# A four-layer graph network on one core: layer 0's table moved to the front of the prologue, edges loaded with groups on partitions

## The chip, the core and the metric

The kernel runs on one core of a Trainium2 chip. A core has five engines that run side by side, each with its own queue of instructions that it works off strictly in order: PE (TensorE, matrix products and transposes), DVE (VectorE), ACT (ScalarE), POOL (GpSimd) and SP (SyncE, which here issues nearly all DMAs). They wait for each other and for DMAs by semaphores. The metric is the device time of one execution in microseconds (us). The profile is one execution taken by the hardware profiler; its span runs from the first to the last instruction.

## The reference

A graph of N = 12,500 nodes and E = 212,500 directed edges, sorted by destination, goes through four layers. Each layer computes `h = relu(layernorm(x))` and adds a message-passing term to `x`:

```
x = x + L0(h, edge_attr_16)   # 4-head attention: softmax over a node's incoming edges
x = x + L1(h, edge_weight1)   # weighted sum over incoming edges, gelu, linear, gelu
x = x + L2(h, edge_attr_9)    # tensor product of rows with edge features, sum
x = x + L3(h)                 # mean over incoming edges, two linears, batch norm
```

Layer 0 is the one that the change is about:

```
Wh = (h @ W.T).reshape(N, 4, 32)
attn = (concat([Wh[src], Wh[dst]], -1) * a).sum(-1)        # per edge and head
attn = leaky_relu(attn, 0.2) + edge_feat @ W_e.T
alpha = segment_softmax(attn, dst)
out = layer_norm(gelu(segment_sum(alpha * Wh[src], dst)))
```

The score splits into a part of the source row and a part of the destination row, so that one table row per node holds what a source gives: 128 numbers of `Wh` and 4 of its part of the score.

## The kernel before

The edges are cut into 208 groups of 1,024 (`GE`; 128 partitions times `T` = 8 slots; the last group is partly filled). Because edges are sorted, the destinations of a group lie in a window of 128 nodes from a first node `base` on.

Before layer 0 there is a prologue (lines 198 to 955), which has no order written out by hand: a scheduler orders each engine's instructions there, and pools of memory decide what may overlap. It has these parts, in this order in the text:

1. Edges (lines 217 to 333). `di` (destinations) and `si` (sources) are loaded as tiles of 128 partitions x 208 groups x 8 slots by `load_edges`, whose pieces are 8 numbers, 32 bytes, each. `ext` takes the largest and smallest destination of each group on each partition, POOL's `partition_all_reduce` makes the maximum over partitions (`red`), `base` comes from it, and `rel` is destination minus `base`. A padded copy of `dst` is made in DRAM (`dpad`), and three shifted copies `seq` of it are read back, from which `bad`, `below` and `units` are made: tests of whether the graph fits the fast path, and where each window of edges begins. `least` and `end` are limits per group, filled by some 60 small memsets. Last, `rel` is transposed in 13 pieces and stored as `rel16` in DRAM.
2. Weights and constants (lines 338 to 423): W0 and the attention vectors become `WE` (128 x 136), the other weights are transposed, `TP` and `mixer` are filled.
3. Layer 0's table (lines 918 to 954): in 25 batches of 4 blocks of 128 nodes, with pools two deep, rows of x are loaded (`xt`), normalised (`norm`, DVE with one square root on ACT), put through relu on ACT, transposed on PE (`pt`), copied by ACT (`hT`), multiplied by `WE` on PE (`pw`), copied out by ACT (`tt`) and DVE (`sd`), and stored by SP as `tab0` (132 numbers a row) and `sdt` (the destination parts, split in three bf16 numbers).

Then layer 0's loop (lines 956 to 1137) runs over the groups in an order written out by hand. For a group g, `load(g)` has SP load edge features, `rel16` rows (`rb`) and a window of `sdt` (`sdw`); `logits(g)` has POOL issue eight indirect DMAs (`gather`, line 661) that fetch 1,024 rows of `tab0` into a row buffer `X`, makes a one-hot matrix `ST` from `rb` (line 1004, DVE), multiplies it by `sdw` on PE, and sums the scores `at` (lines 1010 to 1013, DVE), which SP stores to `lgt` (line 1015). `weights` computes the softmax for four groups at a time. Seven groups later (`LAG`) `spread_out` multiplies the rows by the weights (`msg`, line 1078, DVE) and PE sums them per node (`pag`). A row buffer is free again after that; there are 15 (`LAG + 8`). They lie in the loop's own pool `e0`, whose memory was the prologue's before. In between, the loop makes steps of `Slots` (tables for layers 1 and 3) and of `node0` (the end of layer 0 for a batch of nodes, stored as `xtab` and `htab`).

Layer 1 starts with a load of all edge weights `eww` (lines 1221 to 1230, again by 32-byte pieces), a memset of `tabS` and gathers of `htab`. Its pools take over the memory of layer 0's loop. Layers 2 and 3 follow in the same way.

Of the kernel before, what the change touches and what calls it, by code (L numbers as in the profile page):

```python
# [26 lines left out]
P = 128  # L27
# [66 lines left out]
def gnn_kernel(ctx: ExitStack, tc, x, src, dst, ef16, ef9, ew, W0, We0, a0, lns, lnb, W1, b1,  # L94
# [102 lines left out]

    si = cst.tile([P, NG, T], I, name="si")
    rel = cst.tile([P, NG, T], F, name="rel")
# [5 lines left out]
    early = ExitStack()  # L205
    tmp = early.enter_context(tc.tile_pool(name="acp", bufs=1))
# [6 lines left out]
    TOT = PADF + NG * GE + P  # L213
    NSG = NG // SG
    NK = -(-NB // NBK)
# [5 lines left out]
    with tc.tile_pool(name="ed", bufs=1) as ep:  # L221
        di = ep.tile([P, NG, T], I, name="di")
        load_edges(di, dst, 0, NG, N, 1)
        load_edges(si, src, 0, NG, 0, 1)
        df = ep.tile([P, NG, T], F, name="df")
        vec.tensor_copy(df, di)

        ends = ep.tile([1, max(PADF, TOT - PADF - E)], I, name="ends")
        vec.memset(ends, -1)
        nc.sync.dma_start(dpad[None, :PADF], ends[:, :PADF])  # L230
        ends2 = ep.tile([1, TOT - PADF - E], I, name="ends2")
        vec.memset(ends2, N)
        nc.sync.dma_start(dpad[None, PADF + E :], ends2)
        cut = max(k for k in range(1, P + 1) if E % k == 0)
        nc.sync.dma_start(dpad[PADF : PADF + E].rearrange("(a b) -> a b", a=cut), dst.rearrange("(a b) -> a b", a=cut))
        ext = ep.tile([P, 2, NG + 1], F, name="ext")
        vec.memset(ext[:, :, NG:], 0.0)
        vec.tensor_reduce(ext[:, 0, :NG], df, AX.X, ALU.max)
        vec.tensor_reduce(ext[:, 1, :NG], df, AX.X, ALU.min)
        vec.tensor_scalar_mul(ext[:, 1, :NG], ext[:, 1, :NG], -1.0)  # L240

        seq = [ep.tile([P, NG * T], I, name=f"seq{k}") for k in (0, 1, 2)]
        for t, k in zip(seq, (0, 1, HALO)):
            nc.sync.dma_start(t, windows(dpad, PADF + k, P, NG * T, NG * T))
        bad = [ep.tile([P, NG * T], F, name=f"bad{k}") for k in (0, 1)]
        vec.tensor_tensor(bad[0], seq[2], seq[0], ALU.is_le)
        vec.tensor_scalar(bad[1], seq[0], float(N), None, op0=ALU.is_lt)
        vec.tensor_tensor(bad[0], bad[0], bad[1], ALU.mult)
        vec.tensor_tensor(bad[1], seq[1], seq[0], ALU.is_lt)
        vec.tensor_tensor(bad[0], bad[0], bad[1], ALU.max)  # L250
        vec.tensor_reduce(ext[:, 0, NG:], bad[0], AX.X, ALU.max)
        red = ep.tile([P, 2, NG + 1], F, name="red")
        pool.partition_all_reduce(red, ext, P, bass_isa.ReduceOp.max)
        base = ep.tile([P, NG], F, name="base")
        vec.tensor_scalar_mul(base, red[:, 1, :NG], -1.0)
        vec.tensor_copy(bi, base)
        vec.tensor_tensor(rel, df, base[:, :, None].to_broadcast([P, NG, T]), ALU.subtract)
        vec.tensor_scalar(widx, base, pcol, None, op0=ALU.add)
        span = ep.tile([P, NG], F, name="span")
        vec.tensor_tensor(span, red[:, 0, :NG], base, ALU.subtract)  # L260
        vec.tensor_copy(xall, span)
        vec.tensor_scalar(xall, xall, 7, None, op0=ALU.logical_shift_right)
        vec.tensor_scalar(xall, xall, 1.0, None, op0=ALU.add)
        vec.tensor_scalar(bi3, base, float(BM), None, op0=ALU.min)
        vec.tensor_scalar(bir, bi, RW - 1, None, op0=ALU.bitwise_and)

        last = base[:, G0 - GM : G0, None].to_broadcast([P, GM, T])
        vec.tensor_tensor(relx, rel[:, G0 - GM : G0, :], last, ALU.add)
        vec.tensor_scalar(relx, relx, W0_ * P - 0.5, 4.0 * P, op0=ALU.is_gt, op1=ALU.mult)
        vec.tensor_tensor(relx, relx, rel[:, G0 - GM : G0, :], ALU.add)  # L270
        most = ep.tile([P, 1], F, name="most")
        vec.tensor_reduce(most, span, AX.X, ALU.max)
        worst = ep.tile([P, 1], F, name="worst")
        vec.scalar_tensor_tensor(worst, red[:, 0, NG:], float(W), most, op0=ALU.mult, op1=ALU.max)

        least = ep.tile([P, NG], F, name="least")
        vec.memset(least, 0.0)
        for k, g in enumerate(done):
            if g + 1 < NG:
                vec.memset(least[:, g + 1 :], float(min(NBK * P * (k + 1), N)))  # L280
        vec.memset(least[:, G0:], float(W0_ * P))
        for k, g in enumerate(done):
            if g + 1 >= G0 and g + 1 < NG:
                vec.memset(least[:, g + 1 :], float(min(NBK * P * (k + 1), N)))
        vec.tensor_tensor(least, base, least, ALU.is_lt)

        end = ep.tile([P, NG], F, name="end")
        vec.memset(end, float(RW - W))
        for k, g in enumerate(done):
            if g + 6 < NG:  # L290
                vec.memset(end[:, g + 6 :], float(NBK * P * (k + 1) + RW - W))
        vec.tensor_tensor(end, base, end, ALU.is_gt)
        vec.tensor_tensor(least, least, end, ALU.max)

        UP = NG * T // P
        edge = ep.tile([P, 2, NW], F, name="edge")
        vec.tensor_copy(edge[:, 0, :], wnode)
        vec.tensor_scalar(edge[:, 1, :], wnode, float(P), float(N), op0=ALU.add, op1=ALU.min)
        below = ep.tile([P, 2, NW, UP], F, name="below")
        for k, at in enumerate((P - 1, 0)):  # L300
            unit = seq[0].rearrange("p (u e) -> p u e", e=P)[:, :, at]
            vec.tensor_tensor(below[:, k], unit[:, None, :].to_broadcast([P, NW, UP]),
                              edge[:, k, :, None].to_broadcast([P, NW, UP]), ALU.is_lt)
        units = ep.tile([P, 2, NW], F, name="units")
        vec.tensor_reduce(units, below, AX.X, ALU.add)
        with tc.tile_pool(name="bgp", bufs=1, space=PSUM) as pp:
            pun = pp.tile([P, 2, NW], F, name="pun")
            pe.matmul(pun.rearrange("p k w -> p (k w)"), ones, units.rearrange("p k w -> p (k w)"),
                      start=True, stop=True)
            vec.tensor_scalar(begin, pun[:, 0, :], float(P), float(E - UN * P), op0=ALU.mult, op1=ALU.min)  # L310
            vec.tensor_copy(units[:, 1, :], pun[:, 1, :])
            vec.tensor_tensor(units[:, 0, :], units[:, 1, :], pun[:, 0, :], ALU.subtract)
        vec.tensor_scalar(units[:, 0, :], units[:, 0, :], UN + 0.5, None, op0=ALU.is_gt)
        many = ep.tile([P, 1], F, name="many")
        vec.tensor_reduce(many, units[:, 0, :], AX.X, ALU.max)
        vec.scalar_tensor_tensor(worst, many, float(W), worst, op0=ALU.mult, op1=ALU.max)
        vec.tensor_scalar(many, base[:, G0 - 1 : G0], BM + 0.5, None, op0=ALU.is_gt)
        vec.scalar_tensor_tensor(worst, many, float(W), worst, op0=ALU.mult, op1=ALU.max)
        vec.tensor_scalar(many, red[:, 0, G0 - GM - 1 : G0 - GM], W0_ * P - 0.5, None, op0=ALU.is_gt)
        vec.scalar_tensor_tensor(worst, many, float(W), worst, op0=ALU.mult, op1=ALU.max)  # L320
        late = ep.tile([P, 1], F, name="late")
        vec.tensor_reduce(late, least, AX.X, ALU.max)
        vec.scalar_tensor_tensor(worst, late, float(W), worst, op0=ALU.mult, op1=ALU.max)
        vec.tensor_copy(rough, worst)
        relf = rel.rearrange("p g t -> p (g t)")
        with tc.tile_pool(name="edp", bufs=2, space=PSUM) as pp:
            for c in range(0, NG * T, P):
                n = min(P, NG * T - c)
                prl = pp.tile([P, P], F, name="prl")
                pe.transpose(prl[:n, :], relf[:, c : c + n], ident)  # L330
                rl = ep.tile([P, P], B16, name="rl", bufs=2)
                vec.tensor_copy(rl[:n, :], prl[:n, :])
                nc.sync.dma_start(rel16[c : c + n, :], rl[:n, :])
    ef16f = ef16.rearrange("e f -> (e f)")
    ef9f = ef9.rearrange("e f -> (e f)")


    WE = cst.tile([P, P + 2 * H], F, name="WE")
    W1T = cst.tile([P, P], F, name="W1T")
    WlT = cst.tile([P, P], F, name="WlT")  # L340
    WrT = cst.tile([P, P], F, name="WrT")
# [578 lines left out]
    with tc.tile_pool(name="p0", bufs=2) as sp, tc.tile_pool(name="p0p", bufs=2, space=PSUM) as pp:  # L920
# [5 lines left out]
        for b0, nb in batches(4):  # L926
# [3 lines left out]
            for _ in norm(sp, xt, nb, h):  # L930
                pass
# [833 lines left out]
```

## Time and profile before

| what | us |
|---|---|
| median of 3 runs (7439.46 to 7453.02) | 7448.18 |
| profiled execution | 7429.66 |
| its span | 7427.8 |
| prologue: start to the first gather of layer 0 | 0 to 231.9 |
| of it the table of layer 0 (first load of x to first gather) | 99.9 to 231.9 |
| layer 0's loop: first gather to last sum of messages | 231.9 to 2495 |
| layer 1's first gather | 2524.9 |

All times inside the profiled execution are counted from the start of its span. A row of a timeline gives the start and the duration of an instruction, its engine, its line and operation, and in brackets how long the engine had been idle and what ended that. "SPq" is the time in which SP issues a DMA, not the time of the transfer. A row of a table of windows gives the stretch, its length, the busy time of PE, of PE's weight loads, of DVE, ACT and POOL with the instructions in brackets, then the clock that was granted to PE (1.00 is full speed), the mean busy share of the DMA engines and the GB/s that they moved. Some records of matrix products and of other instructions are missing, so counts are taken from DMA issues.

### The profile page before, as it was taken

Reading aid. Unit: us, or ns where it says so; the run is one execution under the profiler, and the core shown is the slowest. Engines: PE = TensorE matmul, PEld = TensorE weight load, DVE = VectorE, ACT = ScalarE, POOL = GpSimd, SP = SyncE. Lnnn points to the kernel's source line nnn. Section 1 sums busy time; section 2 is a strip of 40 time slices with the busy share of each in tenths; the row PEclk is TensorE's granted clock in tenths of the full one; section 3 lists DMA queues with packets and bytes.
Section 4 is the critical chain, followed back from the end, with each engine's and each line's share of the span. In section 5 each row is a group of like instructions: output and inputs, shape, how many; then the busy total and the mean of one; then the engine's idle time right before and its main releaser. Section 6 shows DMA issues by size and latency. Waiting matters only on the chain.

```text
span 7427.8 us, 119421 instructions
## 1 busy us (share of the span) xinstructions
PE 5056.1 (68%) x39957; PEld 3687.5 (50%) x39958; DVE 5283.1 (71%) x10506; ACT 2841.6 (38%) x7693; POOL 5145.2 (69%) x5372
## 2 busy tenths in 40 slices
PE   3344445444444499888987787778787758788787
PEld 2344444344444366555656777777777732222222
DVE  5678888888888445544448999999999944545454
ACT  1244444444444234434443333333333314444443
POOL 0577777777775377777737777777777767777772
PEclk8566666666666699999987888888888868888887
DMA  5444444444443433333322222222222244344333
GB/s 84 96 105 103 104 106 105 107 106 103 105 105 94 84 88 96 95 90 94 93 72 57 67 71 66 68 69 67 70 69 66 69 126 105 105 106 105 102 103 108
DMA packets 741279, 674.54 MB, mean 91 GB/s; under 512 B 341283, under 2 KB 629398, under 8 KB 740631
## 3 DMA queue, kind: packets, MB, share of 16 engines
q0 software_dynamic: 186624, 382.17, 21.4%
q1 hardware_dynamic: 554027, 284.63, 15.0%
q8 instruction: 316, 5.18, 0.3%
q14 instruction: 312, 2.56, 0.1%
HBM read 603.91 MB, written 63.28 MB: 90 GB/s over the span
## 4 chain that ended last, share of the span: by engine, by line
PE 26%; POOL 16%; DVE 10%; issue 9%; DMA 3%; ACT 1%; DVEq 1%; SPq 0%; POOLq 0%; ACTq 0%
POOL X L661 15%; PE pw L1181 5%; PE px L1200 5%; PE px L1443 4%; PE pw L1429 4%; PE pag L1275 3%; PE pg L1544 3%; DMA X<-htab,si 2%; DVE oh L680 1%; POOL X L669 1%; DVEq L692 1%; PE pag L1332 1%; DVE oh L676 1%; DVE f L1536 1%; DVE B L1314 1%
## 5 line engine op out<-in xcount | busy, mean ns | idle before, releaser
L661 POOL DMA_INDIRECT X<-tab,si x1664 | 1635.6, 983 | 531.0 <-issue 473.0
L661 POOL DMA_INDIRECT X<-htab,si x1664 | 1574.0, 946 | 533.7 <-issue 509.7
L669 POOL DMA_INDIRECT xg<-tab,si x968 | 919.7, 950 | 358.9 <-issue 127.3
L669 POOL DMA_INDIRECT X<-htab,si x968 | 937.1, 968 | 324.2 <-issue 83.8
L1082 PE MATMUL pag<-oh,msg 128*128 128x128 f32 x3328 | 670.5, 383 | 357.4 <-DVE msg L1078 328.7
L1082 PEld LDWEIGHTS pag<-oh,msg 128*128 128x128 f32 x3328 | 620.3, 288 | 373.7 <-DVE msg L1078 336.5
L1454 ACT CAST xb<-px 128x384 bf16<-128x384 f32 x1050 | 501.3, 478 | 737.4 <-PE px L1443 722.0
L1212 ACT ACTIVATE xs<-px,wslot 128x128 f32<-128x128 f32 x1050 | 382.6, 367 | 774.7 <-PE px L1200 698.2
L1332 PE MATMUL pag<-oh,A 128*128 128x128 f32 x3328 | 561.4, 341 | 0.0
L1544 PE MATMUL pg<-xg,oh 128*128 128x385 bf16 x968 | 370.9, 388 | 256.4 <-DVE f L1537 194.9
L1275 PE MATMUL pag<-oh,X 128*128 128x128 f32 x1936 | 432.6, 309 | 165.5 <-DVE acc L1268 121.6
L1332 PEld LDWEIGHTS pag<-oh,A 128*128 128x128 f32 x3328 | 543.5, 256 | 0.0
L1181 PE MATMUL pw<-ohb,xs 128*128 128x128 f32 x2100 | 541.3, 342 | 0.0
L1307 ACT ACTIVATE A<-X,ef 128x128 f32<-128x128 f32 x1664 | 509.9, 391 | 15.7 <-DMA X<-htab,si 15.4
L676 DVE TENSOR_TENSOR oh<-iop,rel 128x1024 f32<-128x1024 f32 (+1 forms) x321 | 388.7, 1211 | 163.2 <-PE pg L1544 162.7
L1200 PE MATMUL px<-tabS,oha 128*32 128x128 f32 x8652 | 488.1, 299 | 5.8 <-ACT xs L1212 5.8
L1071 ACT ACTIVATE oh<-iop,far 128x128 f32<-128x128 f32 x1664 | 451.6, 382 | 48.9 <-DVE ohj L879 38.7
L1181 PEld LDWEIGHTS pw<-ohb,xs 128*128 128x128 f32 x2100 | 334.4, 200 | 219.8 <-issue 218.0
L1334 ACT COPY R<-pag 128x256 f32<-128x256 f32 x208 | 77.4, 372 | 955.6 <-PE pag L1332 955.6
L1332 PE MATMUL pag<-oh,B 128*128 128x128 f32 x3328 | 437.8, 288 | 0.0
L1275 PEld LDWEIGHTS pag<-oh,X 128*128 128x128 f32 x1936 | 326.3, 212 | 206.6 <-DVE acc L1268 139.6
L1332 PEld LDWEIGHTS pag<-oh,B 128*128 128x128 f32 x3328 | 427.3, 208 | 0.0
(460 smaller groups left out, 10444.9 us busy)
## 6 DMA issues: line engine op xcount, KB each, us to landing
lob<-lo SPq DMA_DIRECT2D x252, 224.0 KB
rb<-rel SPq DMA_DIRECT2D x208, 256.0 KB
X<-htab,si POOLq DMA_INDIRECT x2632
X<-tab,si POOLq DMA_INDIRECT x1664
xtab<-xv SPq DMA_DIRECT2D x72, 256.0 KB
xv<-xtab SPq DMA_DIRECT2D x72, 256.0 KB
xg<-tab,si POOLq DMA_INDIRECT x968
lob<-lo SPq DMA_DIRECT2D x84, 160.0 KB
```

What stands on the lines that cost most here:

```text
L661: pool.indirect_dma_start(out=t[:, s, :], out_offset=None, in_=table[:, :], in_offset=bass.IndirectOffsetOnAxis(ap=idx[:, s : s + 1], axis=0))
L669: pool.indirect_dma_start(out=ts[-1][:, : table.shape[1]], out_offset=None, in_=table[:, :], in_offset=bass.IndirectOffsetOnAxis(ap=idx[:, ...
L676: vec.tensor_tensor(s, iop[:, None, :].to_broadcast([P, T, W]), r[:, :, None].to_broadcast([P, T, W]), ALU.is_equal)
L1071: act.activation(S[:, t, :], iop, AF.Abs, bias=far[:, t : t + 1])
L1082: pe.matmul(pag, msg[:, t, :], S[:, t, :], start=t == 0, stop=t == T - 1)
L1181: pe.matmul(pw, x, b, start=j == 0, stop=j == NT - 1)
L1200: pe.matmul(px[q * SL : (q + 1) * SL, :], a[:, jj * P + q * SL : jj * P + (q + 1) * SL], tabS[:, blk, :], start=True, stop=True)
L1275: pe.matmul(p, r[t], s[:, t, :], start=t == 0, stop=t == T - 1)
L1307: act.activation(A[:, t, :], X[:, t, :], AF.Copy, scale=e[:, t, 0:1])
L1332: pe.matmul(pag[: TPK[c] * HD, c, :], lhs, S[:, t, :], start=t == 0, stop=t == T - 1)
L1454: act.copy(x[:, : 3 * P], px)
L1544: pe.matmul(p, s[:, t, :], r[t], start=t == 0, stop=t == T - 1)
```

## The change

Nothing of the result is computed in another precision or left out. The prologue is rewritten; from the loop of layer 0 on, only the pool of the row buffers differs.

- Layer 0's table comes first. Six loads of x open SP's queue, W0 and the attention vectors follow, and rows of x are loaded six batches ahead. The subtraction of the mean and the scaling move from DVE into four ACT instructions per batch (`Relu` with a bias and a scale per partition; DVE makes `mr` for it). The copies `tt` out of PSUM move from ACT to DVE. The parts `sdall` are collected for all nodes, split once, and stored as `sdt` with two DMAs instead of 26.
- Edges are loaded with groups on partitions: 104 groups of 1,024 numbers, 4 KB a row, in two halves (`gs`, `gd`). `si` and `rel` are made from them by 32 PE transposes and 8 DVE copies; POOL turns the sources into floats. Minimum and maximum per group are plain reductions along the row, and four small products by a matrix of ones spread them over the partitions, in place of POOL's `partition_all_reduce`. `rel16` is made by two ACT copies and two stores instead of 13 transposes, copies and stores. `seq` is loaded from `dst` directly.
- The memsets of `least`, `end`, `ends` and of layer 0's `acc` move from DVE to POOL. `bad` becomes bf16 and is evaluated late.
- The row buffers `X` come from a pool `xr` of their own, opened before the prologue's pools and closed after layer 0.

```diff
+    xr = rows_.enter_context(tc.tile_pool(name="xr", bufs=LAG + 8))
+    sp, pp = (pre.enter_context(p) for p in (tc.tile_pool(name="p0", bufs=3),
+                                             tc.tile_pool(name="p0p", bufs=2, space=PSUM)))
+    def rows0(k):
+        if k < NK:
+            b0, nb = k * NBK, min(NBK, NB - k * NBK)
+            xs0[k] = sp.tile([P, nb, D], F, name="xt", bufs=7)
+            load_rows(xs0[k], x, b0, nb)
+    for k in range(6):
+        rows0(k)
...
+    for t, fill in [(gs[1], 0), (gd[1], N)] + [(t, N) for t in seq]:
+        pool.memset(t, fill)
+    for t, v in ((gs, src), (gd, dst)):
+        nc.sync.dma_start(t[0], v[: HG * GE].rearrange("(g e) -> g e", g=HG))
+        nc.sync.dma_start(t[1][: HG - 1], v[HG * GE : (NG - 1) * GE].rearrange("(g e) -> g e", g=HG - 1))
+        nc.sync.dma_start(t[1][HG - 1 : HG, :tail], v[None, (NG - 1) * GE :])
+    def slots_of(out, t, c):
+        for q in range(0, T, 4):
+            ps = ppt.tile([P, 4, HG], F, name="pst")
+            for k in range(4):
+                pe.transpose(ps[:, k, :], t[:, q + k :: T], ident[:HG, :HG])
+            vec.tensor_copy(out[:, c * HG : (c + 1) * HG, q : q + 4].rearrange("p g t -> p t g"), ps)
+    for c in (0, 1):
+        gsf = ep.tile([HG, GE], F, name="gf", bufs=2)
+        pool.tensor_copy(gsf, gs[c])
+        slots_of(si, gsf, c)
+    for k in range(NK):
...
+        act.activation(rs, mv[:, :, 1], AF.Sqrt, bias=eps)
+        vec.reciprocal(rs, rs)
+        mr = sp.tile([P, nb], F, name="mr")
+        vec.scalar_tensor_tensor(mr, mv[:, :, 0], -1.0, rs, op0=ALU.mult, op1=ALU.mult)
+        for j in range(nb):
+            act.activation(h[:, j, :], xt[:, j, :], AF.Relu, bias=mr[:, j : j + 1], scale=rs[:, j : j + 1])
...
+        act.copy(hT, pt)
+        for a in range(0, nb, 2):
+            pw = pp.tile([P, 2, WN], F, name="pw")
+            for j in range(n):
+                pe.matmul(pw[:, j, :], hT[:, a + j, :], WE, start=True, stop=True)
+            vec.tensor_copy(tt[:, a : a + n, :], pw[:, :n, : P + H])
+            vec.tensor_copy(sdall[:, b0 + a : b0 + a + n, :], pw[:, :n, P + H :])
+        store_rows(tab0, tt, b0, nb, P + H)
+        rows0(k + 6)
...
+    store_rows(sdt, s3.rearrange("p j k h -> p j (k h)"), 0, NB, 3 * H)
...
-        load_edges(di, dst, 0, NG, N, 1)
-        load_edges(si, src, 0, NG, 0, 1)
...
-        pool.partition_all_reduce(red, ext, P, bass_isa.ReduceOp.max)
...
+            vec.tensor_reduce(ext[:, c, 0:1], gf[c], AX.X, ALU.min)
+            vec.tensor_reduce(ext[:, c, 1:2], gf[c], AX.X, ALU.max)
+                vec.tensor_scalar(dg, ident[:HG, :HG], ext[:, c, k : k + 1], None, op0=ALU.mult)
+                pe.matmul(pr[:, k, c * HG : (c + 1) * HG], ones[:HG, :], dg, start=True, stop=True)
+            vec.tensor_scalar(gf[c], gf[c], ext[:, c, 0:1], None, op0=ALU.subtract)
...
+        act.copy(r16, gf[c].rearrange("g (p t) -> g t p", t=T))
+        nc.sync.dma_start(rel16[c * HG * T : (c + 1) * HG * T, :].rearrange("(g t) p -> g (t p)", t=T),
+                          r16.rearrange("g t p -> g (t p)"))
+        slots_of(rel, gf[c], c)
...
-    vec.memset(acc.t, 0.0)
+    pool.memset(acc.t, 0.0)
...
-            X = xs[g] = sp.tile([P, T, P + H], F, name="X", bufs=LAG + 8)
+            X = xs[g] = xr.tile([P, T, P + H], F, name="X")
...
+    rows_.close()
```

## The prediction

> **What bounds the kernel now.** First the page: the chain that ended last has PE 26%, POOL 16%, DVE 10%, spread over all four layers. The change touches what lies before layer 0's loop, one stretch on every path, so what counts is when that loop starts, and whether its end moves with its start. The timeline gives the first:
>
> ```profile
> 1.27 15.61 SPq L128 DMA_DIRECT2D si<-in_src_dram  x1
> 34.04 1.03 DVE L226 CAST df<-di 128x1664 f32<-128x1664 int32 x1 [18.74 <-DMA di<-in_dst_dram]
> 67.63 11.45 SPq L333 DMA_DIRECT2D rel<-rl  x13
> 99.91 0.38 SPq L158 DMA_DIRECT2D xt<-in_x_dram  x1
> 140.03 2.18 PE L940 MATMUL pw<-WE,hT 128*128 128x136 f32 x8 [0.73 <-ACT hT L936]
> 143.25 1.11 PE L934 MATMUL pt<-ident,h 128*128 128x128 f32 x4 [1.04 <-ACT h L455]
> 145.10 2.18 PE L940 MATMUL pw<-WE,hT 128*128 128x136 f32 x8 [0.73 <-ACT hT L936]
> 231.89 1.29 POOL L661 DMA_INDIRECT X<-tab,si  x1 [18.97 <-DVE cut_s L975]
> 248.65 0.47 DVE L1004 TENSOR_SCALAR ST<-rb,pcol 128x1024 bf16<-128x1024 bf16 x1
> ```
>
> 32-byte pieces keep DVE waiting until 34 us; `rel16` goes out until 79; the table only begins at 99.9, and its batches follow each other every 5.07 us (140.03 to 145.10). The first gather comes at 231.9, group 1's one-hot at 248.65. The windows of the table stage say what its PE costs:
>
> ```profile
> 110.00:115.00 5.00, 3.98 (x23) 3.33 (x21) 4.23 (x30) 2.67 (x8) 0.00 (x0) 1.00 0.32 93
> 150.00:160.00 10.00, 6.60 (x24) 5.15 (x24) 6.75 (x41) 3.77 (x11) 0.00 (x0) 0.50 0.45 112
> ```
>
> The granted clock is 1.00 in the first 12 us of products and 0.50 later. No engine is over 70% busy at 150: batches wait for each other's results.
>
> Is the loop paced by POOL's gathers (8 per group, 1.25 us apart, 10 us a group) or by its own chain? Counting score stores (one per group) and gathers to the same time decides it:
>
> ```profile
> L1015 SPq DMA_DIRECT2D lgt<-at x16: 319/320/425, 244.7 to 399.6; - x16
> L661 POOL DMA_INDIRECT X<-tab,si x133: 940/944/1777, 231.9 to 399.3; - x133
> L1015 SPq DMA_DIRECT2D lgt<-at x194: 319/320/436, 244.7 to 2311.0; - x194
> L661 POOL DMA_INDIRECT X<-tab,si x1611: 940/944/2173, 231.9 to 2310.8; - x179
> DVE at L1011 <- DMA X<-tab,si: 23.5, 16, 5.7
> ```
>
> At 400 us 16 groups are scored and 16.6 gathered; at 2311, 194 and 201.4. The loop takes 10.74 us a group ((2311 - 399.6) / 178), the gathers 10.3: rows run ahead up to the 15 buffers, and DVE waits for them only 23.5 us in all, nearly all early (last row, from the waits of DVE). So the loop's own chain, DVE at 85%, sets its end, and what counts is when the loop starts, not when the gathers do. Layer 1's start has a cost of its own:
>
> ```profile
> 2495.31 0.10 POOL L134 MEMSET eww<- 128x8 f32 x1 [22.30 <-PE pag L1082]
> 2496.93 13.39 SPq L136 DMA_DIRECT2D eww<-in_edge_weight_dram  x1
> 2508.22 1.13 ACT L455 ACTIVATE t<-h 128x512 f32<-128x512 f32 x2 [0.91 <-DVE h L451]
> 2519.41 1.40 SPq L150 DMA_DIRECT2D htab<-t  x3
> ```
>
> `eww` waits for layer 0's last product (their memory is shared); SP is then held 13.4 us, and the last `htab` rows, ready at 2509.4, go out at 2519.4.
>
> **The change, part by part.** Terms go against the profiled execution, 7429.66 us, 18.5 below the median of the runs; I carry the same difference over to the median.
>
> *Table stage.* Per batch DVE loses the scaling (1.11) and the split (five at 0.17) and gains `mr` (0.17) and two `tt` copies. No row has DVE copy 128x264 from PSUM; from 128x8 (0.158) and 128x128 (0.291) it is 0.44. Sum: statistics 0.87 + 0.36, reciprocal and `mr` 0.34, copies 0.88 + 0.32 = 2.77 us. ACT: root 0.30, four relus 1.20 (the loop's eight 128x128 ACT instructions take 2.17), `hT` 0.59 = 2.09. PE: 1.11 + 2.18 = 3.29 at clock 0.50. In the new PE order batches go in pairs, and PE waits for `hT` twice a pair, about 0.5 and 0.8: 7.9 us a pair. Then: `eps` is there at 9.95 as before, root, relu, transposes and `hT` put the first product at 14; four batches at full clock, 2.8 each as at 110 to 116, give 25. Next PE's order holds the 16 transposes of `si` (4.5), 12 of three batches (3.3), four waits for DVE's copies of them (2.4) and three batches' products (6.5): 42. Nine pairs: 71, 113. Eight transposes of `rel` and the small products for min and max: 3. The last `tt` copy comes at 116, the first gather 4 us later, at 120. Bounds: DVE alone, 14 + 25 x 2.77 + 10 for `si`, `gf`, minima: 93. The old pace: 42 + 18 x 5.07 + 3 = 136. I take 116, as PE's rows are nearest.
>
> The granted clock is the row that this hangs on. "TensorE: Matmul & The Clock Gate" of the Trainium skill, section "What's actually happening", says the reverse: throttled by default, released by activity. By that rule a pair would be held by DVE, 5.5 us, the table would be ready 21 us sooner, and the total 7321; this case shows 1.00 when idle and 0.50 when busy, and I go by that.
>
> *Edges.* 4 KB rows replace the 32-byte pieces; the 34 us at the start disappear behind the table stage. SP issues about 106 DMAs instead of 137 before the loop, at 0.42 each 45 us, in the 120 us that the table takes. POOL gets `acc` (1.9 by the slope of its memsets), `gs`, `gd`, `seq`, `ends` (7), two conversions to float (no row: 0.95 each as a memset to 2.2 as its select) and 60 small memsets (8): done by about 40 us, hidden by the table; uncovered they would cost some 22.
>
> *After the table.* Behind the last `tt` DVE still has, before group 0's one-hot: split, `base`, `rel` copies 5.6; the 208-wide work and `relx` 4; `below`, `units` and a PE wait 5.2; `bad` 10.5 (bf16 products taken like f32, 1.89); maxima 2.3; `TP` 3.8; weights and small constants 2.3; start of `mixer` 2.1 and waits 0.8: 36.6. Such rows overlap (62.3 to 69.1 us: 8.9 in 6.9), so I take 33 (28 to 36.6). SP is not later: its one `sdt` store (issued 4.5 after the table, when the split is made) has 12,416 pieces; `di`'s 26,496 held SP 15.6, so 7.3, then some 22 issues: `rb` and `sdw` at 26 after the table. From group 0's one-hot to group 1's DVE has the rest of `mixer` (7.9), `at` (0.8) and the first slot step (3.6): 12. Group 1's one-hot then comes at 116 + 45 = 161, not 248.65: 88 us earlier. Gathers of the first four groups are done by then, so of DVE's 17 us of later waits for rows I take 10 as saved (0 to 17): other waits take their place.
>
> *Row buffers.* Without their own memory the gathers would wait for the prologue's end. At the other end, `eww` now lies over row buffers read last by group 196, and no longer waits for PE: SP can take it at about 2476 (old times), is free by 2492, and the last `htab` store goes out at 2511 instead of 2519: 8 us (0 to 9). From layer 1 on orders and tiles are the same, so nothing gives the gain back.
>
> Sum: 88 + 10 + 8 = 106. 7429.66 - 106 = 7324 for a profiled execution, 7342 for the median. Ends: 106 + 23 + 5 + 7 + 1 = 142 (7306), 106 - 20 - 4 - 10 - 8 = 64 (7384).
>
> **The rivals.** (1) *PE does not hold the table; DVE does* (ready at 93). For: PE waits 1.3 us a pair only if the order runs as I read it. Against: clock 0.50. Gain 129: 7319. (2) *The old pace stays*, 5.07 a batch, because the engines wait in order for each other: DVE sees `tt` wait for PE with statistics queued behind, which relu waits for. Gain 86 less half the row waits: 7367. (3) *The gathers are not freed*: something in POOL's queue (the last `xt` memset stands ahead of them) or in memory still holds them to the prologue's end at 116 + 45. Group 0's scores come 23 later, the row waits stay: 7375. Against: `xr` is opened first and shares nothing. (4) *Slower: the one `sdt` store.* It replaces 26 that ran beside the table by one in front of `sdw`, on which group 0's product waits. Lower bound 7.3 us; upper from the store of 512 pieces issued at 226.5 and landed by 231.0: 4.5, mostly latency, times 24 is 109. At about 110 the loop starts as late as now; from 130 the 18 us of the other terms are used up too; at 150, 7468. "DMA: Bandwidth & Descriptors", section "Specifications", has pieces under 512 B read, modified and written; doubling 7.3 gives an estimate of 14.6, still hidden behind DVE's 33, so 7342 stands; no row here shows it.
>
> **How the numbers follow.** The forecast case has 0.62 (own range 7320 to 7364), rival 1 0.15, rival 2 0.14, rival 3 0.05, rival 4 0.04. With the run spread of 7 us around the ends, 7306 to 7386 holds 8 in 10. Under 0.2% (15 us) a measurement can't tell a change from none: faster 0.95, same 0.01, slower 0.04.
>
> **What would show it.** Right: first gather near 120, group 1's one-hot near 161; clock 0.50 from about 26 us; PE over 75% busy from 45 to 113; 10.7 us a group in the loop, with fewer than 10 us of waits for rows; `eww` issued before the last message product. Wrong: `sdw` landing long after `rb`; a loop of over 11 us a group; DVE idle on PE for over 2 us a batch.

## The result: 7,427 us instead of the 7,342 predicted

| what | before | after |
|---|---|---|
| median of 20 runs, us | 7440.5 (7424.9 to 7453.0) | 7427.0 (7409.3 to 7439.3) |
| after / before | | 0.9982 (95%: 0.9975 to 0.9990) |
| profiled execution, us | 7429.66 | 7423.80 |
| first gather of layer 0 | 231.9 | 199.7 |
| group 1's one-hot | 248.65 | 251.88 |
| first store of scores | 244.7 | 246.5 |
| last message product's input `msg` | 2491.9 | 2474.3 |
| layer 1's first gather | 2524.9 | 2508.6 |

The kernel is faster by 0.18%, 13.5 us, where 106 were forecast and 7306 to 7386 us was the range for the time. The loop of layer 0 does not start earlier at all: group 1's one-hot is 3 us later than before. What was gained was gained inside the loop.

### The profile page after: what moved, and what is told of

The parts are those of the page before. It is cut to its first block, busy times and chain, and to the rows that moved or that the text cites. A ratio compares the mean times of both kernels' runs of the same rounds, so it can differ in the third digit from the quotient of the medians.

```text
span 7422.0 us, 119285 instructions
## 1 busy us (share of the span) xinstructions
PE 5047.1 (68%) x39986; PEld 3683.5 (50%) x39987; DVE 5260.1 (71%) x10301; ACT 2858.4 (39%) x7719; POOL 5166.8 (70%) x5440
## 4 chain that ended last, share of the span: by engine, by line
PE 27%; POOL 25%; DVE 19%; issue 14%; DMA 9%; ACT 2%; SPq 2%; DVEq 2%; POOLq 0%; ACTq 0%
POOL X L759 23%; PE pw L1246 5%; PE px L1265 5%; PE px L1508 4%; PE pw L1494 4%; PE pag L1340 3%; DMA X<-tab,si 3%; PE pg L1609 2%; DMA X<-htab,si 2%; DMA tab<-tt 2%; PE pag L1145 1%; DVE oh L778 1%; POOL X L767 1%; DVEq L790 1%; DVE msg L1141 1%
## 5 line engine op out<-in xcount | busy, mean ns | idle before, releaser
L1340 PE MATMUL pag<-oh,X 128*128 128x128 f32 x1936 | 435.2, 310 | 165.9 <-DVE acc L1333 122.0
```

The costliest lines, as they stand in the source:

```text
L1340: pe.matmul(p, r[t], s[:, t, :], start=t == 0, stop=t == T - 1)
```

## The profile after

The rows of the timeline that answer to those shown of before:

```profile
199.72 1.12 POOL L759 DMA_INDIRECT X<-tab,si  x1 [81.22 <-DMA WeB<-in_L_gnn_W_e_dram]
```

```profile
251.88 0.58 DVE L1067 TENSOR_SCALAR ST<-rb,pcol 128x1024 bf16<-128x1024 bf16 x1
```

Next, the chain that ended last, over the first 300 us (start, duration, what held it):

```profile
24.99 15.86 SPq L251
40.95 14.38 DMA tab<-tt
...
69.16 33.20 DMA tab<-tt
...
111.29 34.09 DMA tab<-tt
...
152.26 32.85 DMA tab<-tt
```

Three times the chain stands on one store of table rows for 33 to 34 us. DVE shows what that does (timeline of DVE). `tt` has three buffers; when their stores do not land, the next copy out of PSUM waits, and with it the whole table:

```profile
102.45 0.43 DVE L295 COPY tt<-pw 128x264 f32<-128x264 f32 x1 [26.79 <-DMA tab<-tt]
...
145.47 0.43 DVE L295 COPY tt<-pw 128x264 f32<-128x264 f32 x1 [28.18 <-DMA tab<-tt]
...
185.21 0.43 DVE L295 COPY tt<-pw 128x264 f32<-128x264 f32 x1 [26.99 <-DMA tab<-tt]
```

SP's queue says what went out just before each of them:

```profile
65.75 0.34 SPq L396 DMA_DIRECT2D seq<-in_dst_dram  x1
69.16 11.31 SPq L150 DMA_DIRECT2D tab<-tt  x2
80.56 17.78 SPq L158 DMA_DIRECT2D xt<-in_x_dram  x2
...
109.51 0.35 SPq L396 DMA_DIRECT2D seq<-in_dst_dram  x1
111.29 20.32 SPq L150 DMA_DIRECT2D tab<-tt  x2
...
149.53 0.34 SPq L396 DMA_DIRECT2D seq<-in_dst_dram  x1
152.26 11.71 SPq L150 DMA_DIRECT2D tab<-tt  x2
164.03 17.14 SPq L397 DMA_DIRECT2D seq<-in_dst_dram  x1
...
199.25 24.23 SPq L150 DMA_DIRECT2D sdt<-s  x2
```

Each stall follows a load of `seq` (L396: 127 rows of 6,656 bytes, 825.5 KB). And the windows show how such a load runs (columns as in the tables of windows before; the last two are the mean busy share of 16 DMA engines and GB/s):

```profile
113.00:117.00 4.00, 2.98 (x22) 2.34 (x21) 3.59 (x22) 3.86 (x12) 0.00 (x0) 1.00 0.08 31
118.00:138.00 20.00, 0.91 (x5) 0.32 (x3) 0.00 (x0) 2.56 (x7) 0.20 (x1) 0.59 0.15 52
154.00:158.00 4.00, 3.65 (x30) 3.24 (x29) 3.64 (x20) 3.86 (x11) 0.00 (x0) 1.00 0.06 27
```

A share of 0.06 is one engine of sixteen, and it moves 27 GB/s: 825.5 KB take 31 us. From 118 to 138 DVE does nothing and PE, ACT and POOL next to nothing (0.9, 2.6 and 0.2 us of 20), while the DMA engines are at 0.15. So the suspicion is that a load of 127 rows runs on a single DMA engine and that table stores, of which a part goes through the same engine, wait behind it.

The loop itself did what was forecast (score stores and gathers counted to 400 and to 2311 us, and DVE's wait for rows):

```profile
L1078 SPq DMA_DIRECT2D lgt<-at x17: 319/320/432, 246.5 to 397.8; - x17
...
L759 POOL DMA_INDIRECT X<-tab,si x152: 940/944/1937, 199.7 to 399.8; - x152
...
L1078 SPq DMA_DIRECT2D lgt<-at x196: 319/320/437, 246.5 to 2310.9; - x196
```

```profile
DVE at L1074 <- DMA X<-tab,si: 2.9, 15, 0.5
```

From group 17 to group 196 it takes 10.69 us a group ((2310.9 - 397.8) / 179), before 10.74. DVE's wait for rows is 2.9 us in all, before 23.5.

## Experiments

Times are medians; "before" beside a run is the kernel before on the same chip.

### Which loads hold the table up

All three kernels are the kernel after with one edit. In e1 the loads of 103, 104 and 127 rows are cut into a multiple of 16 rows and the rest; the loads of a single row stay as they are.

```diff
+    def spread(t, v, n):
+        m = n // 16 * 16
+        nc.sync.dma_start(t[:m], v[:m])
+        if n > m:
+            nc.sync.dma_start(t[m:n], v[m:n])
...
-        nc.sync.dma_start(t[0], v[: HG * GE].rearrange("(g e) -> g e", g=HG))
-        nc.sync.dma_start(t[1][: HG - 1], v[HG * GE : (NG - 1) * GE].rearrange("(g e) -> g e", g=HG - 1))
+        spread(t[0], v[: HG * GE].rearrange("(g e) -> g e", g=HG), HG)
+        spread(t[1], v[HG * GE : (NG - 1) * GE].rearrange("(g e) -> g e", g=HG - 1), HG - 1)
...
-        nc.sync.dma_start(t[:n], dst[at : at + n * NG * T].rearrange("(p e) -> p e", p=n))
+        spread(t, dst[at : at + n * NG * T].rearrange("(p e) -> p e", p=n), n)
```

> The kernel after, with the loads of 103, 104 and 127 rows (gs, gd, seq) cut in two: first a multiple of 16 rows (96 or 112), then the rest (7, 8 or 15). The tail loads of a single row stay. Theory A (a load whose number of rows has no common divisor with 16 engines' worth of spreading runs on one DMA engine at about 27 GB/s, and the tab0 stores issued later wait behind it there): DVE's four waits of 92 us for tab stores go to under 10, SP is never held over 5 us by a tail load, the last tt copy comes at 93 to 118 instead of 195, the first gather at 97 to 122 instead of 200, and the time falls by 70 to 105 us, to about 7340 (7322 to 7357). Rival B (the single-row tail loads, at which SP is seen held 8, 16 and 17 us, are the cause): those are unchanged, so the waits stay and the time is 7427. Rival C (the stalls go, but the loop's end is set by something that does not move with its start): first gather near 110 and still 7410 to 7430.

In e2 only the last of these edits is made, for `seq`.

> As the kernel after, with only the three seq loads cut in 112 + 15 rows; gs and gd keep their 103 rows. Theory A: the three waits of 27 to 28 us (at 75, 117 and 158 us) go, the one around 30 to 55 us stays; last tt at about 113 to 125, time about 7427 - 80 = 7347 (7335 to 7362). If the three waits came from gs and gd instead, nothing changes.

In e3 `seq` is cut at 122 rows in place of 112:

```diff
-        nc.sync.dma_start(t[:n], dst[at : at + n * NG * T].rearrange("(p e) -> p e", p=n))
+        rows2d, m = dst[at : at + n * NG * T].rearrange("(p e) -> p e", p=n), 122
+        nc.sync.dma_start(t[:m], rows2d[:m])
+        nc.sync.dma_start(t[m:n], rows2d[m:n])
```

> As the kernel after, with the seq loads cut in 122 + 5 rows, so that the large part has 2 as the only common divisor up to 16. Theory A says two engines, some 15 us for 806 KB in place of 31, and so each of the three waits of 27 us shrinks by about 16 to some 11: time about 7427 - 48 = 7379 (7368 to 7392). Rival (any odd shape is slow, or the number of DMAs matters and not the number of engines): either no change, or all of the gain of the cut in 112 + 15.

| | after (above) | e3: 122 + 5 | e2: 112 + 15 | e1: gs, gd too |
|---|---|---|---|---|
| last `tt` copy, us | 194.7 | 133.4 | 111.1 | 93.1 |
| first gather | 199.7 | 149.9 | 115.9 | 96.7 |
| layer 1's first gather | 2508.6 | 2452.1 | 2431.8 | 2407.0 |
| median (before: 7429.1) | 7427.0 (before: 7440.5) | 7366.6 | 7328.6 | 7327.4 |
| ratio, 95% | 0.9975 to 0.9990 | 0.9894 to 0.9944 | 0.9848 to 0.9889 | 0.9831 to 0.9878 |

DVE's waits for table stores in the table stage (sum, number of waits, longest), first of after, then of e3, then of e2:

```profile
DVE tt L295 <- DMA tab<-tt: 92.2, 4, 28.2
```

```profile
DVE tt L295 <- DMA tab<-tt: 31.1, 3, 11.7
```

```profile
DVE tt L301 <- DMA tab<-tt: 10.3, 1, 10.3
```

In e1 there is none. How the large part of `seq` runs, first in e3 (122 rows, nearly alone), then in e2 (112 rows, with other transfers beside it):

```profile
112.00:118.00 6.00, 0.00 (x0) 0.00 (x0) 0.00 (x0) 1.54 (x1) 0.00 (x0) 0.90 0.13 53
```

```profile
66.00:70.00 4.00, 3.25 (x13) 2.85 (x13) 2.65 (x19) 2.81 (x7) 0.00 (x0) 0.50 0.94 273
```

And the load of 103 rows in after:

```profile
22.00:24.00 2.00, 2.00 (x10) 2.00 (x10) 1.10 (x6) 1.64 (x5) 0.38 (x2) 1.00 0.06 25
```

The medians of e2 and e3 lie 6 and 1 us below what was expected; those ranges were counted from 7427 and from a kernel before of 7440.5, which took 7429.1 here. The three waits of 27 us belong to `seq`, as they go in e2. The fourth, of 10.3, stays in e2 and goes in e1, so it belongs to `gs` and `gd` together; no run parts these two. Single-row loads, still there in e1, hold nothing up, so rival B falls. Rival C falls too: layer 1's first gather moves 101.6 us from after to e1, with the first gather's 103.0. And e3 gives the size: one of its three waits is that of `gs` and `gd`, so the three loads of 122 rows leave two waits, of 9.1 and 11.7 us, instead of three of 27, and 112 + 15 leaves none. Alone, a load of 127 rows shows a DMA share of 0.06 and 27 GB/s, one of 122 rows 0.13 and 53, that is one and two engines of sixteen; with 112 rows nearly all are in use (0.94). The number of engines that a load runs on goes by its number of rows. The Trainium skill says how: "DMA: Bandwidth & Descriptors", section "Why a DMA increments its semaphore by 16 and not by 1", has the load split over the largest number of engines up to 16 that divides the slowest dimension of both sides. By that, 127 and 103 rows run on one, 122 on two, 112 on sixteen. These runs agree with it at all of these: in after, from 22 to 24 us, with the load of 103 rows of `gs` under way, the share is 0.06 and the rate 25 GB/s. That a table store is late because a share of it goes through the same engine, and not because it stands behind the load in SP's queue, no run shows by itself; for the `sdt` store, s5 (below) shows a transfer of one queue holding up those of another.

Layer 1's first gather comes 25 us earlier in e1 than in e2, yet the medians are 1.2 apart. The rest, from there to the end of the span, takes 4918.9 us in e1's profiled execution and 4892.9 in e2's; in all other kernels of this study with the kernel before at some 7430 us it lies between these without order. What the medians say to within 10 us, this scatter can hide; the milestones in the trace are the finer measure.

### The suspected cause put into the kernel before

```diff
-            nc.sync.dma_start(t, windows(dpad, PADF + k, P, NG * T, NG * T))
+            nc.sync.dma_start(t[: P - 1], windows(dpad, PADF + k, P - 1, NG * T, NG * T))
+            nc.sync.dma_start(t[P - 1 :], windows(dpad, PADF + k + (P - 1) * NG * T, 1, NG * T, NG * T))
```

> The kernel before, with its three seq loads of 128 rows cut in 127 + 1 rows, nothing else. Theory A: the three loads then take 31 us each on one DMA engine, one after the other, 93 us from 40 us on, where the profile of before has them done some 15 us after issue; the rel stores, the first x loads and all tests on seq wait for them, the first gather comes 50 to 85 us later (280 to 317) and the time is 7490 to 7525. Rival (the number of rows does not matter): 7440, within the spread of runs.

One run took 7515.7 us, 86.5 more than before (7429.1). The first gather is at 320.7 instead of 231.9, 4 us past the expected range. SP's queue and a window of this kernel:

```profile
55.08 32.08 SPq L245 DMA_DIRECT2D seq<-dpad  x1
87.20 0.25 SPq L244 DMA_DIRECT2D seq<-dpad  x1
87.49 31.74 SPq L245 DMA_DIRECT2D seq<-dpad  x1
```

```profile
60.00:70.00 10.00, 0.00 (x0) 0.00 (x0) 0.00 (x0) 0.00 (x0) 0.00 (x0) 1.00 0.06 26
```

The same bytes, with 127 rows in place of 128, run at 26 GB/s on one engine, and SP is held 32 us at the next DMA. One row less in each of three loads costs 86.5 us, most of the 106 that the change was to gain.

### The sdt store

With the loads cut, last `tt` copy to group 0's one-hot is 48 us, and the one store of `sdt` stands in the middle of it. First, ACT issues it in place of SP (edit on e1):

```diff
-    store_rows(sdt, s3.rearrange("p j k h -> p j (k h)"), 0, NB, 3 * H)
+    for b, n, r in rows(0, NB):
+        nc.scalar.dma_start(
+            sdt[b * P : b * P + (n - 1) * P + r, :].rearrange("(j p) d -> p j d", p=r),
+            s3.rearrange("p j k h -> p j (k h)")[:r, b : b + n, :])
```

> The kernel of e1, with the one sdt store (12,416 pieces of 24 bytes) issued by ACT, which is idle then, in place of SP. In e1 SP is held 22.8 us by it (97.1 to 119.9), DVE waits 18.2 us for a seq tail queued behind it, and the first score store comes 56 us after the last tt copy (149.0 against 93.1). Theory A (what is queued behind the store on SP is late, not the transfer itself): DVE's wait of 18 us goes, the first score store comes at 131 to 136, and the first gather of layer 1 moves from 2407 to about 2392; time about 7312 (7300 to 7322). Rival B (the 24-byte pieces keep all 16 DMA engines busy, so that the seq tail, TP and the window sdw land late whoever issues the store): first score store within 4 us of 149, time that of e1, 7327.

When this run, e6 and e7 (below) were taken, the kernel before took 10,223 us and they 10,090, 10,102 and 10,119. Four more (r1, r5, r6, r7: the kernels of e1, e5, e6 and e7) were taken on another chip with before at 10,201. What is different there is told at the end. In r5 the first score store came later than in r1 (224.1 against 204.3) and layer 1's first gather at the same time (3337.4 against 3336.5). s1 and s5 are the same pair of kernels, e1 and e5, with before at 7433.8.

> The kernel of e1, the base for the two beside it. On a chip like that of e1: before 7429, this 7327, first score store 56 us after the last tt copy, 2225 us from it to the last message product, 33 from there to layer 1's first gather. On one like those of e5 and r1: before about 10,200, this about 10,080.

> As e5: the sdt store issued by ACT. On a chip like that of e1: theory A (what is queued on SP behind the store is late) says first score store 11 to 18 us earlier than s1's, and layer 1's first gather too, time 7309 to 7316; rival B (the 24-byte pieces keep the DMA engines busy whoever issues them) says within 4 us of s1. On a chip like that of r1, as there: no gain.

s1 took 7323.5 us (ratio 0.9828 to 0.9861), s5 7314.6 (0.9822 to 0.9855). Group 0's one-hot is at 143.4 and 141.8, layer 1's first gather at 2411.5 and 2411.6: no difference where the store acts, so the 9 us between the medians are not its doing. SP's queue in s1, then ACT's and SP's in s5:

```profile
98.55 22.49 SPq L150 DMA_DIRECT2D sdt<-s  x2
```

```profile
98.68 22.93 ACTq L312 DMA_DIRECT2D sdt<-s  x2
```

```profile
98.00 27.91 SPq L471 DMA_DIRECT2D WeB<-in_L_gnn_W_e_dram  x8
```

Rival B holds: freed of the store, SP is held 27.9 us at the next loads instead. So it is the transfer of the 12,416 pieces that holds the others up, whoever issues it.

Then the store in five parts inside the table stage (edit on e1, in part):

```diff
+        if k % SB == SB - 1 or k == NK - 1:
+            sd, s3, c = sds[k // SB], s3s[k // SB], k // SB * SB * NBK
...
+            store_rows(sdt, s3.rearrange("p j i h -> p j (i h)"), c, b0 + nb - c, 3 * H)
```

> The kernel of e1, with sdt split and stored in five parts of five batches each while the table is made, so that behind the last tt copy only the last part (18 blocks, 2,304 pieces) is left. Theories A and B both: SP is held some 4.5 us after the table in place of 22.8; the parts cost DVE about 5 times 2.2 us less what the whole split costs now, and hold SP 4 times 4.6 us beside the table, which DVE paces at 9 us busy in 10. Last tt copy at 93 to 103, first score store at 131 to 142 in place of 149.0; time 7309 to 7322. If the parts hold up the tab stores in the table stage (their pieces in front of them on all engines), last tt later than 105 and no gain.

> As e6. The last tt copy was at 103.9 there, where e5 had 94.6: the parts cost the table stage some 10 us. So by A and B: SP held 4.5 us after the table in place of 22.8, first score store 0 to 10 us earlier than r1's, time 7317 to 7327.

It ran only where before takes 10,200 us: r6 took 10,082.2 us against r1's 10,074.2 beside it. The last `tt` copy came at 106.9 instead of 92.1, the first score store at 201.0 instead of 204.3, layer 1's first gather at 3348.2 instead of 3336.5. The parts slow the table by 14.8 us and save 18.1 behind it, and yet layer 1's first gather is 11.7 later; why is open. With before at 7430 us this was not tried.

Last, the store put behind all other loads of the prologue (edit on e1):

```diff
-    store_rows(sdt, s3.rearrange("p j k h -> p j (k h)"), 0, NB, 3 * H)
...
+    store_rows(sdt, s3.rearrange("p j k h -> p j (k h)"), 0, NB, 3 * H)
     pre.close()
```

> The kernel of s1, with the sdt store moved in SP's queue behind the seq tail, the loads of WeB, TP and the other weights, directly ahead of the loop's loads. s1: last tt copy 94.6, DVE idle 17.8 us behind the store, group 0's one-hot at 143.4, layer 1's first gather at 2411.5, 7323. If the prediction's 33 us of DVE work after the table (28 to 36.6) were right and only the store's 22 us on the DMA engines hide it, DVE's wait of 18 us goes, its block is done by 128 to 131, and what then counts is the store itself: about 13 us of other issues, 22 for the store, rb and sdw behind it: group 0's one-hot at 136 to 140, layer 1's first gather 3 to 7 us earlier, time 7316 to 7321. If the block is longer than predicted by itself, DVE is still at work at 135 and the one-hot comes at 143 or later.

t8 took 7323.1 us (before 7424.2; ratio 0.9840 to 0.9871), the same as s1, but group 0's one-hot is at 152.4, where 136 to 140 was expected, and layer 1's first gather at 2419.0, 7.5 later, where 3 to 7 earlier was expected. DVE's timeline and SP's queue:

```profile
116.53 25.07 SPq L150 DMA_DIRECT2D sdt<-s  x2
```

```profile
145.50 0.06 DVE L1033 MEMSET z<- 128x4 f32 x1 [23.45 <-DMA sdt<-s]
```

DVE had done what it had to do ahead of the loop at 122.0, 27 us after the last `tt` copy (94.9). But the loop's pools lie over the store's source, and their first memset waits until the store has been read. So the block of DVE work was predicted too long rather than too short, and what makes it 48 us is the store: SP is held 22 to 25 us by it, and behind it wait `TP`, the `seq` tail and the loop's memory.

### The row buffers alone

X goes back into the loop's pool, on e1 (the pool `xr` is no longer opened):

```diff
-            X = xs[g] = xr.tile([P, T, P + H], F, name="X")
+            X = xs[g] = sp.tile([P, T, P + H], F, name="X", bufs=LAG + 8)
```

> The kernel of e1, with the row buffers X back in the pool of layer 0's loop, whose memory the prologue uses. The prediction had gathers that run ahead worth 10 us of waits for rows (0 to 17) and the earlier eww worth 8 (0 to 9). The profile of after has the loop, from first score store to last message product, 2228 us long against 2247 before, and the way from there to layer 1's first gather 34.3 against 33.0, so that all of it lies in the rows and nothing in eww. By the profile: first gather at 130 to 138 instead of 97, loop 2240 to 2250 instead of 2225, first gather of layer 1 18 us later (2420 to 2430), time 7345 (7335 to 7357). By the prediction's split: 10 of the 18 in the loop, 8 behind it. If the buffers are worth nothing: 7327.

> As e7: X back in the loop's pool. On a chip like that of e1: first gather 130 to 141 instead of 97, loop 2240 to 2250 us instead of 2225, layer 1's first gather 18 us later than s1's, time 7345 (7335 to 7357); by the prediction's split 10 in the loop and 8 behind it. On a chip like that of r1, 34 us later as there.

s7 took 7344.7 us against s1's 7323.5 (ratios to before 0.9867 to 0.9900 and 0.9828 to 0.9861). First gather 141.5 instead of 98.7; first score store 153.9 instead of 150.1; from there to the last `msg` 2243.0 instead of 2228.5; from `msg` to layer 1's first gather 34.0 instead of 32.9; sum 19.4. DVE's waits for rows, in s7 and in s1:

```profile
DVE at L1078 <- DMA X<-tab,si: 24.3, 18, 5.0
```

```profile
DVE at L1080 <- DMA X<-tab,si: 1.7, 8, 0.5
```

Beside r1 the same edit cost 42 us (r7: 10,115.8 against 10,074.2). So, with before at 7430 us, the buffers of their own are worth some 20 us: 18.3 up to the last `msg`, where the waits for rows differ by 22.6, and 1 us behind it.

## Why the prediction was wrong, point by point

| step | predicted | after | s1 (loads cut) |
|---|---|---|---|
| last `tt` copy | 116 | 194.7 | 94.6 |
| from there to group 0's one-hot | 33 | 44.6 | 48.8 |
| group 1's one-hot | 161 | 251.88 | 153.7 |
| group 1's one-hot to last `msg` (before 2243.3) | 10 less | 20.9 less | 18.4 less |
| last `msg` to layer 1's first gather (before 33.0) | 8 less | 1.3 more | 0.1 less |

*The step that failed* is in "Edges": "4 KB rows replace the 32-byte pieces; the 34 us at the start disappear behind the table stage. SP issues about 106 DMAs instead of 137 before the loop, at 0.42 each 45 us". It counted the new loads by their issue and by the size of their pieces, and never asked how long each transfer takes and what shares its engines. "Nine pairs: 71, 113" then took for granted that table stores land in time. Five loads of 103 and 127 rows ran on one DMA engine at 27 GB/s instead; DVE waited 92.2 us for stores behind them, and the table ended 79 us late. e1 to e4 show this from both sides. The rivals of the prediction had a late store, but the wrong one.

*The pace of the table* was wrong as well, the other way. With the loads cut, the last copy comes at 93 to 95, the bound that the prediction had given for DVE alone (rival 1), not at 116. The step was "clock 0.50 from about 26 us". In s1 the windows give:

```profile
60.00:92.00 32.00, 24.97 (x166) 19.64 (x166) 29.20 (x167) 30.92 (x81) 0.20 (x1) 1.00 0.87 230
...
98.50:121.00 22.50, 0.72 (x2) 0.50 (x2) 6.54 (x21) 0.00 (x0) 13.10 (x13) 0.50 1.40 44
```

PE is busy 78% of 60 to 92 at clock 1.00, and idle from 98 to 121 at 0.50. (A DMA share over 1, as here, comes of counting a packet's whole time in the stretch in which it starts.) That is the way round that the Trainium skill's "TensorE: Matmul & The Clock Gate", section "What's actually happening", states it and the prediction rejected: throttled by default, released by activity. The 1.00 that the prediction read in an idle prologue lies before the first record of a clock in the trace (at 111.8 us in before, when PE was already at work), so it is no sign that idleness gives the full clock. How busy PE must be is not settled here: in before the clock stayed at 0.50 from 150 to 160, with PE busy 66%. ACT at 97% and DVE at 91% hold the stage. A row of ACT's groups from 60 to 92 in s1:

```profile
L289 ACT ACTIVATE h<-xt,mr,rs 128x128 f32<-128x128 f32 x53 | 21.8, 483 | 0.0
```

Four relus take 1.65 us of ACT (21.8 / 53, times 4) where the prediction had 1.20, and 26 copies `tt`, two a batch, leave 2.46 us a batch (rival 2's old pace was 5.07). So ACT is the busiest engine there, and that the sum for DVE alone, with 2.77 a batch, came out at 93 is in part luck.

*After the table*: 33 was DVE's work; in t8 this takes 27, and in s1 29 (48.8 less waits of 17.8, 1.7 and 0.3). What was mis-sized is the `sdt` store: 7.3 us, by the rate of 32-byte pieces that are loaded, became 22 to 24; the other end named, 109, was far off. Per piece SP is held 1.8 ns (22.5 / 12,416) against 0.59 for `di`'s (15.6 / 26,496), three times as much. The Trainium skill's "DMA: Bandwidth & Descriptors", section "Specifications", has pieces under 512 bytes read, modified and written, from which the prediction made an estimate of 14.6; the direction agrees, the size does not, and no run shows the reading and writing back itself. As in rival 4 the store sits in front of `sdw`, with a fifth of the 110 us from which that rival decides.

*The loop's end moves with its start*: right. First score store to last `msg` is 2227.8 in after, 2225.0 in e1, 2231.5 in e2, 2224.3 in e3, with starts 98 us apart.

*Waits for rows*: rival 3 fell, as in s1 the first gather comes 4 us after the last `tt` copy (98.7 and 94.6). Predicted 10 of 17, "other waits take their place". They do not: nearly all 20 us come through (after 2.9 us of waits, before 23.5; s7 gives them back). In after this is the whole of the gain.

*eww*: predicted 8 us, measured about 1 (32.9 in s1 from the last `msg` to layer 1's first gather, 34.0 in s7). The step said that its memory is read last by group 196. The timeline of after shows it waiting for the last `msg`:

```profile
2474.31 1.21 DVE L1141 TENSOR_TENSOR msg<-X,alp 128x1024 f32<-128x1024 f32 x1
2475.55 1.93 SPq L128 DMA_DIRECT2D eww<-in_edge_weight_dram  x2
...
2477.54 13.36 SPq L136 DMA_DIRECT2D eww<-in_edge_weight_dram  x1
```

It no longer waits for PE, only for DVE right ahead of PE, and the 13.4 us of SP still follow.

Sum for after, to layer 1's first gather: 3.2 later at group 1's one-hot, 20.9 less in the loop, 1.3 more behind it: 16.4 earlier, as measured (2524.9 to 2508.6). For s1: 95.0 + 18.4 + 0.1 = 113.4. That the version with the loads cut ends at 7323 to 7327, near the 7342 foretold for after, is in part luck: a table 21 us faster and rows 8 better stand against a block 16 longer and 8 us of `eww` that did not come.

The version that beats both kernels is e1: 7327.4 and, as s1, 7323.5 us, 1.5% below before.

## What to carry to other kernels

Cost a DMA by the number of engines that it runs on, not only by its bytes and pieces: take row counts with 16 as a divisor, and put the rest into a DMA of its own. A large load on one engine is dangerous for what is queued behind it: here table stores took 33 to 34 us to land behind loads of 31 us. Before moving loads beside a stage that streams through few buffers, list the transfers that its buffers wait for.

## What the hardware showed that was not expected

- One engine moves 26 to 28 GB/s (after, e4), and while it is behind, SP itself is held 8 to 32 us at a later DMA, a load of 2 KB on a single row among them (15.86 us at L251).
- Stored pieces of 24 bytes hold the issuing queue three times as long as loaded ones of 32 bytes do, 22.5 us for 290 KB (s1), and they hold up the DMAs of other queues (s5: 27.9 us at SP while ACT issued the store).
- In layer 3 the same 7,297 recorded products kept PE busy 1,064.6 us in e2 and 1,086.8 in s1 (granted clock 0.84 and 0.82), and the layer took 1,387 and 1,410 us. Most of the scatter between runs lies there; why the clock differs is open.
- Beside e5 to e7 and r1 to r7 all kernels took 10,070 to 10,220 us. A gather takes 944 to 947 ns there as elsewhere, but the granted clock is 0.71 instead of 0.79, and there are pauses between instructions that the profile puts down to "remote", as in this row of r1's DVE timeline:

```profile
160.95 0.23 DVE L514 SCALAR_TENSOR_TENSOR row<-one,here,row 128x15 f32<-128x15 f32 x1 [4.11 <-remote]
```

  Why is open. It need not be the chip: e5 to e7 and s1, s5, s7 and t8 are recorded under the same chip number, with before at 10,223 and at 7424 to 7434. The cut loads gained 127 us there (10,201.2 to 10,074.2), 102 and 110 elsewhere.
